# A row transform and an inverse product whose tables move from the streamed to the stationary operand, with two turns through device memory

## The chip, the cores and the metric

The kernel runs on one core of a Trainium2 chip. The metric is device time in microseconds (us); less is better. Engines are named as the profile names them: PE is the matrix engine (PEld its weight loads), DVE the vector engine, ACT the scalar engine, POOL the general engine, SP the engine that here issues most DMAs (SPq its queue).

## The reference

For each of 64 images of 96 channels and 56 x 56 pixels, three layers run one after the other:

```
L0 conv:  1x1 expand to 192, BN, SiLU, shift, shuffle; depthwise 3x3 + identity, SiLU;
          squeeze-excite gate; 1x1 project to 96, BN, + x, SiLU            -> t
L1 attn:  LayerNorm over channels, h = relu(BN(LN(t) @ w1.T))               (3136 tokens x 192)
          X = fft(h over the 3136 tokens, ortho)
          Xr' = relu(Xr*rd - Xi*id + rb) etc. (per channel, shrunk),  y = ifft(..).real
          t = t + BN(y @ w2.T)
L1 ffn:   LayerNorm, fp8 (e5m2) quantised 96 -> 384 -> 96 with fp16 accumulation, + t
```

The transform of length 3136 is done as 56 x 56: a transform along one index of 56 (the row transform, step `f1`), a product with a table that holds the twiddles and the second transform (`f2`), the per-channel part, the product with `w2`, and then the inverse in two steps, `i1` and `i2`. Because the input is real, only NK = 29 of the 56 first frequencies are kept.

## The kernel before

One image is one batch `b` of the plan, and all of its work is cut into small steps (`ea_mm`, `dw_mm`, `f1_mm`, ...). A step is a Python function `step(b, i)` that issues a few instructions. `PLAN` holds a time for every step and part; at the end of the kernel the pairs (batch, step) of all 64 batches are sorted by `b * PERIOD + when`, and issued in that order. The numbers in `PLAN` are therefore only an order; every engine then takes its own instructions strictly in that order, and waits where an operand is not ready. One period holds steps of three or four different batches: the convolution of batch b+1 (`ea`, `eb`, `dw`, `pj`, `c`), the transform of batch b (`w1`, `f1`, `f2`, `w2`, `i1`, `i2`), and the normalisation and the quantised layer of batches b-1 and b-2 (`n`, `x`, `h`, `o`).

The steps that the change touches, in the order of the data:

- `w1_mm`, `w1_ev` (L649, L661): product with `w1` on PE, then DVE writes `relu` times the row scale into `buf_h`, seen as `h_v`.
- `f1_mm`, `f1_ev` (L676, L688): row transform. A slice of `buf_h` of one channel (128 partitions x 56 columns) is the stationary operand, the table `f_tab` (58 columns) is streamed. There are 6 parts of 16 x 2 products. The result comes out turned, with the other pixel index on the partitions, and ACT copies it into `buf_g`, seen as `g_v`.
- `f2_mm`, `f2_u`, `f2_s`, `f2_r`, `f2_p`: the second transform with `l_tab` (L703, L713), then ACT and DVE work; the result goes to `buf_h` as `pq_a` and `pq_b`.
- `w2_mm`, `w2_ev` (L768, L780, L798): product with `w2`; ACT writes `buf_g` as `u_v`.
- `i1_mm`, `i1_ev` (L809, L820): inverse product. Slices of `u_v` (112 x 32) are stationary, `inv_tab` (56 columns) is streamed, in 3 parts of 64 products; ACT copies the turned result into `buf_h` as `p_v`.
- `i2_mm`, `i2_ev` (L831, L844): second inverse product with `r_tab`, added to `t`.

`buf_h` and `buf_g` exist once, so `w1` of the next batch can write only after `i2` of this batch has read. PSUM tiles of these steps alternate between two buffers (`mix_ps`); the other steps share four (`psb`). SP issues the loads of the next image (`x_in`, L192), the output stores (`o_st`, L932) and one small row copy (`sp_ev`, L635).

## Time and profile before

| | |
|---|---|
| time, median of 3 runs | 7428.37 us (7425.02 to 7429.1) |
| span of the profiled execution | 7414.7 us, clock 0.993 |
| PE busy | 7188.3 us (97%), 177666 instructions |
| PEld busy | 5229.7 us (71%) |
| DVE, ACT, POOL busy | 4842.3 (65%), 4641.4 (63%), 1589.9 us (21%) |
| chain that ended last | PE 93%, ACT 3%, issue 3%, DVE 1% |
| DMA | 185.34 MB, mean 25 GB/s |
| `f1_mm` on PE (L676) | 24576 matmuls, 675.6 us |
| `i1_mm` on PE (L809) | 24576 matmuls, 373.3 us, 99.3 us idle before |
| `f1_ev` on ACT (L688), `i1_ev` (L820) | 388.8 us, 176.2 us |

The span runs from the first to the last instruction of one profiled execution; the time of a run lies 13.7 us above it, for what lies around. Busy time of a group is the time in which at least one of its instructions ran; matmuls overlap, so it is far less than the count times the duration of one. "Idle before" is the time for which the engine stood still just ahead of instructions of that group, with the one that ended the wait behind the arrow.

### The profile page before, as it was taken

The numbers are of one execution on the slowest core, as the hardware profiler recorded it, in microseconds if no ns is written. First come the engines' busy times: TensorE is split into PE (matmuls) and PEld (weight loads), VectorE is DVE, ScalarE is ACT, GpSimd is POOL, SyncE is SP. The second block draws the span as 40 slices with busy tenths as digits, with TensorE's granted clock in tenths as the row PEclk, the third lists the DMA queues.
The fourth block names the chain that finished last, engine by engine and source line by source line (L and its number), as shares of the span: only waits on it lengthen the run. The fifth ranks groups of instructions, "written<-read, shape, count | busy, mean of one in ns | idle before, by whom it ended". The sixth has DMA issues, their size and how long they took to land.

```text
span 7414.7 us, 383547 instructions
## 1 busy us (share of the span) xinstructions
PE 7188.3 (97%) x177666; PEld 5229.7 (71%) x177666; DVE 4842.3 (65%) x8790; ACT 4641.4 (63%) x9806; POOL 1589.9 (21%) x1366
## 2 busy tenths in 40 slices
PE   7999999999999999999999999999999999999997
PEld 5777777777777777777777777777777777777775
DVE  5666667666666666666666666666666666666674
ACT  3566666566665666666656666566666666666665
POOL 1221222212212122122121221221212212212222
PEclk9999999999999999999999999999999999999998
DMA  2010110110101101011011011110110111101100
GB/s 52 18 28 20 28 27 19 28 24 23 28 20 28 26 20 28 21 27 28 18 29 26 20 28 23 25 27 19 30 26 20 28 23 24 28 20 28 27 20 21
DMA packets 424334, 185.34 MB, mean 25 GB/s; under 512 B 378786, under 2 KB 422042, under 8 KB 422474
## 3 DMA queue, kind: packets, MB, share of 16 engines
q1 hardware_dynamic: 420794, 159.01, 9.3%
q8 instruction: 1392, 22.81, 1.3%
q0 software_dynamic: 528, 1.50, 0.1%
q14 instruction: 212, 1.73, 0.1%
q10 hardware_dynamic: 1408, 0.28, 0.0%
HBM read 82.80 MB, written 77.07 MB: 22 GB/s over the span
## 4 chain that ended last, share of the span: by engine, by line
PE 93%; ACT 3%; issue 3%; DVE 1%; POOL 0%; DMA 0%; POOLq 0%; ACTq 0%; SPq 0%
PE ps_d L469 14%; PE psa L676 9%; PE psa L649 9%; PE ps_ea L406 5%; PE ps_eb L423 5%; PE psa L831 5%; PE ps_n L580 5%; PE ps_pj L555 5%; PE psa L768 5%; PE psa L809 4%; PE ps_c L580 4%; PE psa L703 4%; PE ps_h L888 4%; PE ps_o L910 3%; PE psa L713 3%
## 5 line engine op out<-in xcount | busy, mean ns | idle before, releaser
L926 POOL TENSOR_TENSOR o<-t,o 112x448 f32<-112x448 f32 x448 | 659.1, 1471 | 3629.9 <-DVE o L920 2280.0
L469 PE MATMUL ps_d<-e_a,diag 32*32 32x392 f32 x36864 | 1029.5, 498 | 0.7 <-ACT d L479 0.7
L898 DVE TENSOR_SCALAR y<-y,qb 128x448 f16<-128x448 f16 x1344 | 483.1, 384 | 761.5 <-ACT y L893 748.4
L491 DVE SCALAR_TENSOR_TENSOR d_last<-e_b,taps,d_last 128x1568 f32<-128x1568 f32 x512 | 972.5, 1899 | 9.3
L469 PEld LDWEIGHTS ps_d<-e_a,diag 32*32 32x32 f32 x36864 | 659.8, 103 | 299.6 <-issue 37.5
L591 DVE TENSOR_REDUCE v<-sq 112x4 f32<-112x384 f32 x896 | 490.6, 548 | 480.7 <-ACT sq L587 479.7
L893 ACT CAST y<-ps_h 128x448 f16<-128x448 f32 x1344 | 682.6, 543 | 165.7 <-PE ps_h L888 157.8
L860 POOL TENSOR_TENSOR rs<-v,mhalf 112x4 f32<-112x4 f32 x448 | 489.5, 1097 | 1264.2 <-DVE v L592 1264.2
L649 PEld LDWEIGHTS psa<-w1c,t 112*64 112x64 f32 x14336 | 609.0, 137 | 178.0 <-issue 86.4
L904 ACT CAST h<-y 128x448 fp8e5<-128x448 f16 x1344 | 733.0, 570 | 2.2 <-DVE y L898 2.0
L676 PEld LDWEIGHTS psa<-f_tab,buf_h 128*56 128x56 f32 x24576 | 650.4, 131 | 111.0 <-ACT buf_g L688 45.4
L649 PE MATMUL psa<-w1c,t 112*64 112x96 f32 x14336 | 688.4, 249 | 3.4 <-DVE buf_h L661 1.8
L676 PE MATMUL psa<-f_tab,buf_h 128*56 128x58 f32 x24576 | 675.6, 216 | 1.1 <-DVE buf_h L661 1.1
L609 POOL TENSOR_TENSOR rs<-v,mhalf 112x4 f32<-112x4 f32 x448 | 461.1, 1034 | 917.2 <-DVE v L592 763.3
L566 DVE TENSOR_TENSOR ps_pj<-ps_pj,x 112x392 f32<-112x392 f32 x512 | 260.6, 566 | 546.0 <-issue 326.1
L572 ACT ACTIVATE t<-ps_pj,pjbn_b 112x392 f32<-112x392 f32 x512 | 289.6, 621 | 413.5 <-DVE ps_pj L566 413.5
L661 DVE SCALAR_TENSOR_TENSOR buf_h<-psa,rs_full 128x768 f32<-128x768 f32 (+1 forms) x512 | 430.8, 852 | 148.7 <-PE psa L649 148.7
L688 ACT COPY buf_g<-psa 128x464 f32<-128x464 f32 x768 | 388.8, 551 | 186.4 <-PE psa L676 184.7
L411 ACT ACTIVATE e_a<-ps_ea 128x448 f32<-128x448 f32 x448 | 237.6, 551 | 427.3 <-PE ps_ea L406 427.2
L809 PE MATMUL psa<-inv_tab,buf_g 112*32 112x56 f32 x24576 | 373.3, 214 | 99.3 <-issue 97.5
L809 PEld LDWEIGHTS psa<-inv_tab,buf_g 112*32 112x32 f32 x24576 | 327.5, 110 | 197.5 <-issue 196.3
L866 DVE TENSOR_TENSOR xt<-ps_n,rs 112x384 fp8e5<-112x384 f32 x448 | 243.7, 556 | 315.8 <-POOL rs L860 311.4
(176 smaller groups left out, 12984.4 us busy)
## 6 DMA issues: line engine op xcount, KB each, us to landing
x<-in_x SPq DMA_DIRECT2D x896, 84.0 KB, 2.7
out_dram<-o SPq DMA_DIRECT2D x896, 84.0 KB, 2.1
l_tab<-in_tab_l SPq DMA_DIRECT2D x1, 1624.0 KB, 6.9
r_tab<-in_tab_r SPq DMA_DIRECT2D x1, 1568.0 KB
t<-dev_t SPq DMA_DIRECT2D x64, 7.0 KB, 1.8
t<-dev_t SPq DMA_DIRECT2D x64, 5.2 KB
ex_row_p<-in_expand_row POOLq DMA_DIRECT2D x1, 336.0 KB, 4.3
s_p<-in_bn POOLq DMA_DIRECT2D x1, 288.0 KB, 4.6
```

The costliest lines, as they stand in the source:

```text
L469: nc.tensor.matmul(pss[r][j * 32 : j * 32 + 32], lhsT=diag[pr, tap, :], rhs=e_a[pr, r0 : r0 + PJ, dx : dx + HW], start=tap == 0, stop=tap ...
L491: nc.vector.scalar_tensor_tensor(d_last, win, w, d_last, ALU.mult, ALU.add)
L580: nc.tensor.matmul(cen[c0:c1, k, 0:C], lhsT=t_of(b)[:, n0 + c0 : n0 + c1], rhs=center, start=True, stop=True)
L591: nc.vector.tensor_reduce(v, sq, AX.X, ALU.add)
L649: nc.tensor.matmul(ps[hc * 64 : hc * 64 + 64, k, 0:C], lhsT=t[:, n0 : n0 + 64], rhs=w1c[:, hc * C : hc * C + C], start=True, stop=True,)
L676: nc.tensor.matmul(ps[r * 64 : r * 64 + HW, k, 0 : 2 * NK], lhsT=buf_h[:, n0 : n0 + HW], rhs=f_tab[:, r, :], start=True, stop=True,)
L809: nc.tensor.matmul(ps[p0 : p0 + 32, k, 0:HW], lhsT=u_v[:, oh * 48 + o, :], rhs=inv_tab[:, r, :], start=True, stop=True,)
L860: nc.gpsimd.tensor_tensor(rs, held.pop(("nv", b, g)), mhalf[0:CP, 0:4], ALU.pow)
L893: nc.scalar.copy(y16, held.pop(("h", b, i)))
L898: nc.vector.tensor_scalar(y16, y16, qb1[:, i % 3 : i % 3 + 1], 0.0, ALU.add, ALU.max)
L904: nc.scalar.copy(held["h8", b, j][:, m, :], held.pop(("y", b, i)), saturate=False)
L926: nc.gpsimd.tensor_tensor(o32, rows, o16, ALU.add)
```

## The change

In `f1` and `i1` the operands trade places: the table becomes the stationary operand and the data are streamed, in `f1` as 7 parts of 4 products of 384 columns on four 64 x 64 corners of the array, in `i1` as 3 parts of 2 products of up to 480 columns on the whole array. The results then do not come out turned. They are turned by writing them to device memory and reading them back: `f1_ev` copies into a new tile `fs` (two buffers), `f1_st` stores it in four DMAs per part, and `f2_ld` loads it into `g_v` in four pieces of four DMAs; `i1_ev` copies into `q_v`, `i1_st` stores it in three DMAs, and `i2_ld` loads `p_v` in two pieces of four DMAs. Ahead of each piece but the first, SP issues a DMA of 4 bytes out of the piece before into a tile `probe`, so that SP waits until that piece has landed. `i2_mm` covers other rows in a part (its count of matmuls is the same), and `r_tab` has another layout of half the size per partition. All times of `PLAN` are new. The one-time loads that POOL issued are issued by ACT. Core of the diff:

```diff
-PERIOD = 116.1319138
+PERIOD = 116.1300000
...
+    "ea_mm": (-134.0591300, -135.8943500, -134.9482400, -82.9315800, -134.3902000, -81.6978800, -73.0405500),
...
+    "dw_mm": (-79.0431300, -76.9247100, -76.4118400, -66.0765200, -63.9181200, -60.6314000),
...
-    "f1_mm": (21.4014670, 24.1096820, 21.6576037, 26.6862219, 27.4741769, 27.9467307),
...
-    "f2_mm": (32.9716451, 29.2956139, 40.4533546, 44.1808546, 54.3439615, 55.8928972),
...
+    "f1_mm": (4.3575000, 6.7899600, 13.2490100, 13.3480500, 26.4222100, 27.3651600, 36.3461700),
+    "f1_ev": (9.9199800, 12.6915700, 15.0915200, 16.8658800, 27.4890500, 27.9876900, 37.4188100),
+    "f1_st": (12.3906800, 15.6355123, 15.8052200, 21.7471100, 30.3743500, 31.4346249, 40.2672500),
+    "f2_ld": (40.4725800, 42.9361900, 44.9466800, 53.7646300),
+    "f2_mm": (40.5122600, 47.0136900, 49.7942100, 50.7436500, 57.9144900, 60.3104800),
...
-    "i1_mm": (80.9444124, 84.7640673, 88.5170591),
-    "i1_ev": (82.2893126, 88.4629084, 91.9656135),
-    "i2_mm": (95.7640245, 96.2774235, 108.3942264, 108.5026333),
...
+    "i1_mm": (78.3167100, 79.8851600, 87.9770000),
+    "i1_ev": (80.3238500, 81.9603700, 83.6106300, 83.8193600, 90.1147200, 90.0279800),
+    "i1_st": (86.9858500, 89.0839200, 95.7684200),
+    "i2_ld": (103.0982000, 105.5906800),
+    "i2_mm": (104.3956884, 104.6307600, 109.4537598, 109.0033800),
...
+    dram = ctx.enter_context(tc.tile_pool(name="dram", bufs=2, space=bass.MemoryType.DRAM))
...
-        nc.gpsimd.dma_start(out=b[0:rows], in_=src.rearrange("(o f) c -> o f c", o=1).to_broadcast([rows, 4, n]))
+        nc.scalar.dma_start(out=b[0:rows], in_=src.rearrange("(o f) c -> o f c", o=1).to_broadcast([rows, 4, n]))
...
-    buf_g = const.tile([128, NK * MID], F32, name="buf_g")
+    buf_g = const.tile([128, (NK + 32) * C], F32, name="buf_g")
...
...
         d, j0, n = W1[g]
         ps = held.pop(("w1", b, g))
         nc.vector.scalar_tensor_tensor(
-            h_v[:, :, d * NJ + j0 : d * NJ + j0 + n],
-            ps[:, 0:n, 0:C].rearrange("p b c -> p c b"),
+            h_v[:, d * NJ + j0 : d * NJ + j0 + n, :],
+            ps[:, 0:n, 0:C],
             0.0,
-            rs_full[:, d, j0 : j0 + n].unsqueeze(1).to_broadcast([128, C, n]),
+            rs_full[:, d, j0 : j0 + n].unsqueeze(2).to_broadcast([128, n, C]),
             ALU.max,
             ALU.mult,
         )
 
 
     def f1_mm(b, g):
-        ps = mix_ps(c=16, k=64)
-        for k in range(16):
-            n0 = (g * 16 + k) * HW
-            for r in range(2):
+        ps = mix_ps(h=2, n=512)
+        for hc in range(2):
+            for d in range(2):
+                n0 = d * NJ + g * 4
                 nc.tensor.matmul(
-                    ps[r * 64 : r * 64 + HW, k, 0 : 2 * NK],
-                    lhsT=buf_h[:, n0 : n0 + HW],
-                    rhs=f_tab[:, r, :],
+                    ps[d * 64 : d * 64 + 64, hc, 0 : 4 * C],
+                    lhsT=f_tab[hc * 64 : hc * 64 + HW, :],
+                    rhs=h_v[hc * 64 : hc * 64 + HW, n0 : n0 + 4, :],
                     start=True,
                     stop=True,
                 )
         held["f1", b, g] = ps
 
-    def f1_ev(b, n):
-        g, hc = divmod(n, 2)
-        c0 = hc * C + g * 16
-        nc.scalar.copy(
-            g_v[:, :, c0 : c0 + 16],
-            held["f1", b, g][:, :, hc * NK : hc * NK + NK].rearrange("p c k -> p k c"),
-        )
+    def f1_ev(b, g):
+        fs = work.tile([128, 4, 2, C], F32, tag="fs", name="fs")
+        ps = held.pop(("f1", b, g))
+        nc.scalar.copy(fs.rearrange("p b h c -> p h b c"), ps[:, :, 0 : 4 * C].rearrange("p h (b c) -> p h b c", c=C))
+        held["fs", b, g] = fs
+
+    def f1_st(b, g):
+        if ("spec", b) not in held:
+            held["spec", b] = dram.tile([4, NJ, 32, MID], F32, tag="spec", name="spec")
+        fs = held.pop(("fs", b, g)).rearrange("p b h c -> p b (h c)")
+        for p in range(4):
+            nc.sync.dma_start(
+                out=held["spec", b][p, g * 4 : g * 4 + 4].rearrange("b k c -> k b c"), in_=fs[p * 32 : p * 32 + 32]
+            )
+
+    LD = ((0, 8), (8, 16), (16, 24), (24, NK))
+
+    def f2_ld(b, i):
+        k0, k1 = LD[i]
+        if i:
+            nc.sync.dma_start(out=probe[0:1, 0:1], in_=g_v[64:65, LD[i - 1][0], 0:1])
+        for r in range(2):
+            for d in range(2):
+                p0 = r * 64 + d * NJ
+                nc.sync.dma_start(out=g_v[p0 : p0 + NJ, k0:k1, :], in_=held["spec", b][d * 2 + r, :, k0:k1, :])
 
 
     F2 = ((fa, pq_a, 0, 8), (fb, pq_b, 0, 8), (fa, pq_a, 8, 8), (fa, pq_a, 16, 8), (fb, pq_b, 8, 7), (fa, pq_a, 24, 5))
...
         if len(low) == len(high) == 4:
             parts = [(ps.rearrange("p u k o -> p (u k) o")[:, :, 0:C], 8)]
         for src, n in parts:
-            nc.scalar.copy(u_v[:, :, at : at + n], src.rearrange("p k o -> p o k"))
+            nc.scalar.copy(u_v[:, at * C : (at + n) * C].rearrange("p (k o) -> p k o", o=C), src)
             at += n
 
 
     def i1_mm(b, g):
-        ps = mix_ps(o=16, b=64)
-        for k in range(16):
-            o = g * 16 + k
-            for oh in range(2):
-                for r in range(2):
-                    p0 = oh * 64 + r * 32
-                    nc.tensor.matmul(
-                        ps[p0 : p0 + 32, k, 0:HW],
-                        lhsT=u_v[:, oh * 48 + o, :],
-                        rhs=inv_tab[:, r, :],
-                        start=True,
-                        stop=True,
-                    )
+        ps = mix_ps(u=2, n=512)
+        for u in range(2):
+            c0 = (g * 2 + u) * 5 * C
+            c1 = min(c0 + 5 * C, NK * C)
+            nc.tensor.matmul(
+                ps[0:CP, u, 0 : c1 - c0],
+                lhsT=inv_tab.rearrange("p r n -> p (r n)"),
+                rhs=u_v[:, c0:c1],
+                start=True,
+                stop=True,
+            )
         held["i1", b, g] = ps
 
-    def i1_ev(b, g):
-        ps = held.pop(("i1", b, g))
-        nc.scalar.copy(p_v[:, :, g * 16 : g * 16 + 16], ps[:, :, 0:HW].rearrange("p o b -> p b o"))
+    def i1_ev(b, n):
+        g, u = divmod(n, 2)
+        c0, c1 = n * 5 * C, min((n + 1) * 5 * C, NK * C)
+        nc.scalar.copy(q_v[:, c0:c1], held["i1", b, g][0:CP, u, 0 : c1 - c0])
+
+    def i1_st(b, g):
+        if ("rows", b) not in held:
+            held["rows", b] = dram.tile([CP, 32 * C], F32, tag="rows", name="rows")
+        cs = slice(g * 10 * C, (g * 10 + 10 if g < 2 else 32) * C)
+        nc.sync.dma_start(out=held["rows", b][:, cs], in_=q_v[:, cs])
+
+    def i2_ld(b, h):
+        ns = slice(h * 14, h * 14 + 14)
+        if h:
+            nc.sync.dma_start(out=probe[0:1, 1:2], in_=p_v[0:1, 0, 0:1])
+        for d in range(2):
+            for r in range(2):
+                p0 = d * 64 + r * 32
+                src = held["rows", b][r * HW : r * HW + HW].rearrange("(n d) (k o) -> d k n o", d=2, o=C)
+                nc.sync.dma_start(out=p_v[p0 : p0 + 32, ns, :], in_=src[d, :, ns, :])
 
 
     def i2_mm(b, g):
         ps = mix_ps(u=2, k=8, a=64)
         for turn in range(2):
             for k in range(7):
-                for bk in range(2):
-                    oh = turn ^ bk
-                    n2 = g * 14 + bk * 7 + k
-                    pr = slice(oh * 64, oh * 64 + 64)
+                for d in range(2):
+                    oh = turn ^ d
+                    pr = slice(d * 64, d * 64 + 64)
                     nc.tensor.matmul(
-                        ps[oh * 64 : oh * 64 + 48, bk, k, 0:HW],
-                        lhsT=buf_h[pr, n2 * 48 : n2 * 48 + 48],
-                        rhs=r_tab[pr, n2, :],
+                        ps[oh * 64 : oh * 64 + 48, d, k, 0:HW],
+                        lhsT=p_v[pr, g * 7 + k, oh * 48 : oh * 48 + 48],
+                        rhs=r_tab[pr, g * 7 + k, :],
                         start=True,
                         stop=True,
                     )
         held["i2", b, g] = ps
 
     def i2_ev(b, n):
-        g, bk = divmod(n, 2)
-        n0 = (g * 14 + bk * 7) * HW
-        cols = t_of(b)[:, n0 : n0 + 7 * HW].rearrange("p (k a) -> p k a", a=HW)
-        nc.vector.scalar_tensor_tensor(cols, held["i2", b, g][0:CP, bk, 0:7, 0:HW], b2_sh, cols, ALU.add, ALU.add)
+        g, d = divmod(n, 2)
+        cols = t_of(b)[:, 0:NPIX].rearrange("p (n d a) -> p n d a", d=2, a=HW)[:, g * 7 : g * 7 + 7, d, :]
+        nc.vector.scalar_tensor_tensor(cols, held["i2", b, g][0:CP, d, 0:7, 0:HW], b2_sh, cols, ALU.add, ALU.add)
 
...
-    f = np.zeros((128, 2, 2 * NK))
+    f = np.zeros((128, 64))
...
-    r = np.zeros((128, HW, HW))
+    r = np.zeros((128, NJ, HW))
...
-    nc = bacc.Bacc("TRN2", target_bir_lowering=False, num_devices=1)
+    nc = bacc.Bacc("TRN2", target_bir_lowering=False, num_devices=1, dynamic_dma_scratch_size=2048)
```

## The prediction, made before the changed kernel ran

> **What bounds the kernel now.** I read the page's first part, then its chain, then the groups kept apart by shape. PE is busy for 97% of the span and 93% of the chain that ended last, and no slice is thin:

> ```profile
> PE 7188.3 (97%) x177666; PEld 5229.7 (71%) x177666; DVE 4842.3 (65%) x8790; ACT 4641.4 (63%) x9806; POOL 1589.9 (21%) x1366
> ...
> PE 93%; ACT 3%; issue 3%; DVE 1%; POOL 0%; DMA 0%; POOLq 0%; ACTq 0%; SPq 0%
> ```

> So PE work taken out is time won, unless PE then waits. The groups of the two steps that change:

> ```profile
> L676 PE MATMUL psa<-f_tab,buf_h 128*56 128x58 f32 x24576 | 675.6, 216 | 1.1 <-DVE buf_h L661 1.1
> L809 PE MATMUL psa<-inv_tab,buf_g 112*32 112x56 f32 x24576 | 373.3, 214 | 99.3 <-issue 97.5 <-ACT buf_g L798 1.0
> L780 PE MATMUL psa<-w2b,buf_h 64*64 64x96 f32 x3712 | 216.6, 251 | 0.0
> L820 ACT COPY buf_h<-psa 128x896 f32<-128x896 f32 x192 | 176.2, 918 | 7.3 <-PE psa L809 7.3
> ```

> Per batch (of 64) `f1` holds PE for (675.6 + 1.1)/64 = **10.6 us** and `i1` for (373.3 + 99.3)/64 = **7.4 us**. The program writes 192 products per batch for each, the trace has 24576/64 = 384: a float32 product is two passes. What a period is worth comes from the gate product, one per batch: (7229.8 - 64.6)/63 = **113.7 us**:

> ```profile
> L540 DVE SCALAR_TENSOR_TENSOR pw<-gate,pj_w x64: 741/742/744, 64.6 to 7229.8; 128x560 f32<-128x560 f32 x64
> ```

> For prices I read PE's timeline of one period (start, length, line, count); a step costs the distance to the next start:

> ```profile
> 2999.62 7.27 PE L469 MATMUL ps_d<-e_a,diag 32*32 32x392 f32 x256
> 3006.82 1.56 PE L713 MATMUL psa<-l_tab,buf_g 128*64 128x112 f32 x28
> ...
> 3014.47 0.89 PE L780 MATMUL psa<-w2b,buf_h 64*64 64x96 f32 x32
> ...
> 3031.22 1.78 PE L809 MATMUL psa<-inv_tab,buf_g 112*32 112x56 f32 x128
> ...
> 3046.85 0.96 PE L406 MATMUL ps_ea<-x,ex_w 112*32 112x448 f32 x8
> 3047.74 2.19 PE L580 MATMUL ps_c<-center,t 112*64 112x96 f32 x48
> 3049.87 0.96 PE L406 MATMUL ps_ea<-x,ex_w 112*32 112x448 f32 x8
> ```

> A `dw` step (96 passes) is 2.7 us, an `f2` part of 16 products (32 passes) 1.7, `c` 0.71, `ea` 0.89; likewise `h` 0.27, `o` 0.67, `eb` 1.4 and `i2` 2.9.

> [...] the trace agrees in `w2` (L780): without the 0.25 us that a single pass takes, (0.89 - 0.25)/31 = 20.6 ns per pass, so four corners of 96 columns in 83 ns. [...]

> **PE work removed.** `f1`: 7 parts x 2 passes = 14 groups of four corners, 384 columns each. At 83 ns per 96 columns that is 332 ns a group, 14 x 0.332 = 4.7 us, so -5.9 us. `i1`: 6 products over 29 x 96 = 2784 columns, two passes, whole array. The trace has no long float32 stream on the whole array; the pair of column tiles in L713 takes 2 x (1.56 - 0.26)/27 = 96 ns for 112 columns, 0.86 ns a column, so 2 x 2784 x 0.86 = 4.8 us. Upper bound: the 12 weight loads of 112 columns (172 ns each in the `pj` group) show in full, 6.9 us; lower bound 4.4, at the 0.79 ns a column of the `pj` passes on four row tiles (32 in 2.90 us: (2.90 - 0.49)/31 x 4/392). I take 4.8: -2.6 us. `i2` keeps its 224 passes on diagonal corner pairs: 0. Sum **-8.45 us per batch, -541 us**: 7428 becomes 6887 if PE never waits anew.

> **Other engines, beside PE.** ACT: `f1_ev` 6.1 us per batch becomes 7 x 0.81 (the 768-column copy of L798) = 5.7; `i1_ev` 2.75 becomes 5 x 0.58 + 0.5 = 3.4; sum +0.2. DVE: `w1_ev` keeps its elements (953 ns now): 0. Against a period of about 108 us ACT comes to 67%, DVE 70%, still under PE. POOL loses only one-time loads; these move to ACT's queue ahead of the first batch: within 5 us either way.

> **SP and the DMAs.** Now 30 DMAs per batch, then 30 + 28 stores + 16 loads + 3 probes + 3 stores + 8 loads + 1 probe = 89. An issue holds SP 0.42 us (output) to 0.67 us (row copy), so some 42 us of a period plus waits: room. Bytes: 2.75 + 2.49 + 1.38 + 1.38 = 8.0 MB more per batch. Today's queue needs 9.3% x 16 x 7414.7 / 420794 = 26 ns per packet; the some 8000 new packets, most of them larger, at 25 to 110 ns come to 35 us of all engines per batch, against today's 10% busy. Bandwidth doesn't bind; the round trips can.

> ```profile
> x<-in_x SPq DMA_DIRECT2D x896, 84.0 KB, 2.7
> out_dram<-o SPq DMA_DIRECT2D x896, 84.0 KB, 2.1
> l_tab<-in_tab_l SPq DMA_DIRECT2D x1, 1624.0 KB, 6.9
> ```

> **The waits added**, by the new order of `PLAN`. Landing prices: 2.1 us for a store, 2.7 for a strided load; bounds 1.8 (best) and 6.1 us (the longest `x` load).
> (a) *`f1_mm(6)` to `f2_mm(0)`*: copy 1.0, four issues 1.8, landing 2.1, four loads of 172 KB (issue 1.8, the last landing 2.8): **9.5 us**. PE has queued between them `dw_mm(0..2)` = **8.1 us**. Stall 1.4, and 0.5 for SP or ACT being late: 1.9. Bounds 0 and 5.
> (b) *`f2_mm(1)`* needs the second piece. SP stands at the probe till the first has landed, then issues: 0.45 + 1.8 + 2.8 = **5.05 us** per piece. On PE: `f2_mm(0)` 1.7, `o` 0.67, `h` twice 0.54, `ea` 0.89 = **3.8**. Stall 1.2; bounds 0 and 3.
> (c) Third and fourth piece: `f2_mm(1)`, `f2_mm(2)`, `dw_mm(3)` and an `h` are 6.4 us against 5.05; `f2_mm(3)` and two `dw` 7.1 against 5.05 plus `o_st(6)`, 0.9. Stall 0; at a cadence of 7 us, 1.5.
> (d) *`i1_mm(2)` to `i2_mm(0)`*: copies 1.3, issue 0.45, landing of 516 KB 3.8, four loads in runs of 384 B (1.9 + 2.7): **10.2 us**. On PE: six `c` 4.3, four `ea` 3.6, `eb` 1.4, two `h` and two `o` 1.9 = **11.1**. Stall 0; bounds 0 and 4. The second load has 6.9 us of PE work against 5.05: 0.
> (e) `fs` has two buffers: `f1_ev(2)` stands behind the landing of `f1_st(0)`, and ACT with it; `w1_mm(5)` waits for that PSUM buffer. 0.4. `w2_mm(3)` now sits just ahead of `i1_mm(2)`: 0.5.
> Behind the waiting SP stand `x_in`, `o_st` and the row copy: the copy for `w1_mm` has 14 us of `i2` and others ahead of it, the rest more.
> Sum of stalls **4.0 us per batch, +256 us**. The first and last batch have little to lay over the turns: +20 us.

> **Sum**: against the profiled run 7414.7 + 13.7 = 7428.4, which is the median: 7428 - 541 + 256 + 20 = **7163 us**, say 7160 (3.6% less).

> **Rivals.** *Turns fully covered*: ACT and SP run ahead, stalls under 2 us; 6890 to 7030, say 6960. For it: (d) has slack. Against: (a) and (b) are short by my prices. *Turns longer than their cover* (the slower side): PE stands at `f2_mm(0)`, `f2_mm(1)` and `i2_mm(0)`. Stores, loads, probes and PE's own instruction fetch (queue q8, 22.8 MB) share 16 engines; with store-to-load trips of 13 us at both turns and 7 us a piece the stalls are 4.9 + 3.2 + 1.5 + 1.9 + 0.9 = 12.4 us, and 7428 - 541 + 794 + 20 = 7700. It decides from 8.1 us of stalls per batch. For it: `i1` already loses 97.5 us to "issue", and the trips are in series. Against: queues are 10% busy now. *Tiles that don't overlap* (the change doesn't do what it says): corners of `f1` in pairs only cost 9.4 us; 7163 + 300 = 7463. Against it is L780.

> **Chances.** Partly covered 0.50 (7030 to 7320), fully covered 0.18, between 7320 and the old time 0.05; same 0.03; slower 0.24 (turns 0.20, tiles 0.04). A difference of 0.2% is about what a measurement of this kernel can tell from no change. Faster 0.73, same 0.03, slower 0.24. The range 6930 to 7540 leaves out about one in twenty below and one in eight above.

> **What would show it.** Right: 3584 matmuls for `f1` and 768 for `i1`, some 300 us busy each; idle time of PE or PEld ahead of `f2` ended by DMA into `buf_g`, some 200 us, and next to none ahead of `i2`; PE share near 93%; period near 109.5 us. Wrong: `f1` near 600 us (tiles), idle time at `f2` over 400 us (turns), or waits of PE for ACT or DVE in the stretch from `f2` to `w2`, where 36 us of ACT work and 30 of DVE stand beside 34 of PE.

## The result, and the profile after

The changed kernel takes **7387.8 us** (median of 4 runs, 7377.8 to 7396.4), the kernel before beside it 7426.7: a ratio of 0.9947 (95% interval 0.9933 to 0.9961). It is 39 us faster where 265 were forecast: clear of the noise, but the sign is all that came out.

The first two lines are from the first part of the page of the changed kernel, the next from its DMA queues, the last is its chain:

```profile
span 7377.8 us, 300741 instructions
...
PE 6817.4 (92%) x132866; PEld 4575.5 (62%) x132866; DVE 4793.1 (65%) x8790; ACT 4638.9 (63%) x9678; POOL 1524.4 (21%) x1355
...
q1 hardware_dynamic: 984506, 670.40, 37.5%
...
PE 48%; DVE 18%; DMA 15%; ACT 10%; SPq 4%; issue 4%; POOL 2%; POOLq 0%; ACTq 0%; DVEq 0%
```

PE lost 371 us of busy time while the span fell by only 37: the rest is now time in which PE stands. Its share of the chain went from 93% to 48%. The granted clock fell from 0.993 to 0.971, which the prediction had not thought of.

The groups of PE with shapes kept apart (columns as before: count, busy us, mean ns, idle before with what ended it):

```profile
L680 PE MATMUL psa<-buf_h,f_tab 56*64 56x384 f32 x3584 | 349.7, 497 | 1.5 <-DVE buf_h L665 1.4
L829 PE MATMUL psa<-buf_g,inv_tab 112*112 112x480 f32 x640 | 294.9, 575 | 0.2 <-ACT buf_g L820 0.2
L829 PE MATMUL psa<-buf_g,inv_tab 112*112 112x384 f32 x128 | 51.6, 485 | 0.0
L725 PE MATMUL psa<-l_tab,buf_g 128*64 128x112 f32 x7424 | 431.2, 269 | 142.6 <-DMA buf_g<-spec 114.2 <-DVE ue L769 9.4 <-ACT h L939 7.8
L735 PE MATMUL psa<-l_tab,buf_g 128*64 128x112 f32 x3840 | 226.1, 264 | 68.5 <-DMA buf_g<-spec 63.4 <-DVE ue L769 4.3 <-issue 0.3
L867 PE MATMUL psa<-r_tab,buf_h 64*48 64x56 f32 x14336 | 360.8, 215 | 91.9 <-DMA buf_h<-rows 76.0 <-issue 13.0 <-DVE dev L620 1.6
L923 PE MATMUL ps_h<-xq,q 96*128 96x448 fp8e5 x1344 | 454.0, 371 | 115.1 <-ACT o L950 113.6 <-ACT y L928 0.6 <-ACT xq L917 0.6
L790 PE MATMUL psa<-w2a,buf_h 128*64 128x96 f32 x3712 | 423.7, 275 | 8.5 <-DVE ue L769 8.4
```

`f1` (L680) and `i1` (L829) have the forecast counts and nearly the forecast time. `f2` (L725, L735) waits 177.6 us for the first turn, `i2` (L867) 76 for the second. Two lines are new surprises: `h_mm` (L923) waits 113.6 us for ScalarE's `o_ev`, and `w2` (L790) has the same instructions as L768 before, but is busy 423.7 us where that was 364.1:

```profile
L768 PE MATMUL psa<-w2a,buf_h 128*64 128x96 f32 x3712 | 364.1, 251 | 1.6 <-DVE ue L747 1.6
```

One period on PE's timeline shows why (start, length, line, count, wait with its releaser):

```profile
3064.70 7.88 PE L473 MATMUL ps_d<-e_a,diag 32*32 32x392 f32 x273
3072.95 0.89 PE L473 MATMUL ps_d<-e_a,diag 32*32 32x392 f32 x15 [0.37 <-issue]
3075.71 1.75 PE L725 MATMUL psa<-l_tab,buf_g 128*64 128x112 f32 x32 [1.87 <-DMA buf_g<-spec]
...
3082.11 0.99 PE L735 MATMUL psa<-l_tab,buf_g 128*64 128x112 f32 x16 [1.65 <-DMA buf_g<-spec]
3083.03 0.36 PE L923 MATMUL ps_h<-xq,q 96*128 96x448 fp8e5 x1
3083.32 3.06 PE L725 MATMUL psa<-l_tab,buf_g 128*64 128x112 f32 x32
...
3101.89 0.35 PE L923 MATMUL ps_h<-xq,q 96*128 96x448 fp8e5 x1 [1.14 <-ACT o L950]
3102.17 0.43 PE L520 MATMUL ps_se<-red,ep_w 24*32 24x1 f32 x32
...
3105.22 1.55 PE L802 MATMUL psa<-w2b,buf_h 64*64 64x96 f32 x32
...
3112.86 0.89 PE L802 MATMUL psa<-w2b,buf_h 64*64 64x96 f32 x32
```

The 32 passes of L725 take 1.75 us at 3075 and 3.06 at 3083; the 32 of L802 take 1.55 us at 3105, soon after a wait, and 0.89 a little later. The clock record has half clock from 3083.58 to 3086.99 and from 3104.06 to 3107.47, and full clock between.

SP's own timeline over the same turn:

```profile
3059.79 9.18 SPq L700 DMA_DIRECT2D spec<-fs  x11
3069.06 3.18 SPq L713 DMA_DIRECT2D buf_g<-spec  x4
3075.41 0.64 SPq L709 DMA_DIRECT2D probe<-buf_g  x1
3076.10 2.45 SPq L713 DMA_DIRECT2D buf_g<-spec  x4
3081.82 0.60 SPq L709 DMA_DIRECT2D probe<-buf_g  x1
```

From the end of `f1_mm(6)` (3064.8) to `f2_mm(0)` (3075.7) the trip takes 10.9 us over 9.1 us of `dw`; a piece takes 3081.82 - 3075.41 = 6.4 us. Four load issues take 3.18 and 2.45 us.

I split every period (53 of them, away from the ends) by the starts of PE's matmuls in the trace: the time to the next start, less the gap in which none ran, at full clock or in a stretch of half clock, and the gaps put to the step that follows them. In us per batch:

| | period | full clock | half clock | idle | of it `f2` | `i2` | `h` | `eb` | `w2` | `i1` |
|---|---|---|---|---|---|---|---|---|---|---|
| before | 114.10 | 111.42 | 0.45 | 2.24 | 0 | 0 | 0 | 0 | 0 | 1.52 |
| after | 112.97 | 100.85 | 5.05 | 7.06 | 3.07 | 1.22 | 1.81 | 0.74 | 0.04 | 0 |
| no turns (`e1`) | 106.84 | 99.60 | 4.43 | 2.81 | 0.70 | 0 | 2.11 | 0 | 0 | 0 |
| no turns, new ACT order (`e10`) | 104.60 | 101.45 | 1.04 | 2.11 | 0.70 | 0 | 0 | 0 | 1.41 | 0 |
| turns, new ACT order (`e5`) | 111.51 | 101.81 | 3.17 | 6.53 | 2.98 | 1.27 | 0.03 | 0.73 | 1.27 | 0 |

Counting half-clock time at half its length, PE's work fell from 111.65 to 103.38 us (-8.27), the loss to the half clock grew from 0.23 to 2.53 (+2.30), and idle time from 2.24 to 7.06 (+4.82): -1.15, but for rounding the 1.13 us by which the period fell. That is 72 us over 64 batches, of which the two ends of the program give 33 back.

### The profile page after: what moved, and what is told of

The parts are those of the page before. It is cut to its first block, busy times and chain, and to the rows that moved or that the text cites. A ratio compares the mean times of both kernels' runs of the same rounds, so it can differ in the third digit from the quotient of the medians.

```text
span 7377.8 us, 300741 instructions
## 1 busy us (share of the span) xinstructions
PE 6817.4 (92%) x132866; PEld 4575.5 (62%) x132866; DVE 4793.1 (65%) x8790; ACT 4638.9 (63%) x9678; POOL 1524.4 (21%) x1355
## 3 DMA queue, kind: packets, MB, share of 16 engines
q1 hardware_dynamic: 984506, 670.40, 37.5%
q14 instruction: 258, 2.11, 0.1%
## 4 chain that ended last, share of the span: by engine, by line
PE 48%; DVE 18%; DMA 15%; ACT 10%; SPq 4%; issue 4%; POOL 2%; POOLq 0%; ACTq 0%; DVEq 0%
DMA buf_g<-spec 7%; PE psa L790 5%; PE psa L653 5%; PE ps_pj L559 5%; PE psa L867 4%; PE psa L829 4%; DVE s L766 4%; DVE ue L769 4%; DMA buf_h<-rows 4%; PE ps_n L584 3%; PE ps_eb L427 3%; PE psa L802 3%; ACT ue L750 3%; DMA spec<-fs 3%; PE ps_c L584 2%
## 5 line engine op out<-in xcount | busy, mean ns | idle before, releaser
L961 POOL TENSOR_TENSOR o<-t,o 112x448 f32<-112x448 f32 x448 | 614.7, 1378 | 4114.1 <-DVE o L955 1565.3
L473 PE MATMUL ps_d<-e_a,diag 32*32 32x392 f32 x36864 | 1075.3, 497 | 3.6 <-issue 3.4
L895 POOL TENSOR_TENSOR rs<-v,mhalf 112x4 f32<-112x4 f32 x448 | 450.5, 1010 | 1195.1 <-DVE v L596 1190.5
L928 ACT CAST y<-ps_h 128x448 f16<-128x448 f32 x1344 | 679.0, 542 | 12.7 <-PE ps_h L923 10.7
L725 PE MATMUL psa<-l_tab,buf_g 128*64 128x112 f32 x7424 | 431.2, 269 | 142.6 <-DMA buf_g<-spec 114.2
L923 PE MATMUL ps_h<-xq,q 96*128 96x448 fp8e5 x1344 | 454.0, 371 | 115.1 <-ACT o L950 113.6
L613 POOL TENSOR_TENSOR rs<-v,mhalf 112x4 f32<-112x4 f32 x448 | 443.7, 1012 | 539.5 <-DVE v L596 536.9
L779 DVE SCALAR_TENSOR_TENSOR buf_h<-ue,s 128x448 f32<-128x448 f32 (+2 forms) x768 | 478.9, 665 | 111.8 <-ACT s L773 111.8
L725 PEld LDWEIGHTS psa<-l_tab,buf_g 128*64 128x64 f32 x7424 | 377.3, 141 | 266.9 <-issue 134.7
L766 DVE SCALAR_TENSOR_TENSOR s<-psa,fa,ue 128x448 f32<-128x448 f32 (+1 forms) x512 | 324.9, 635 | 273.9 <-ACT ue L750 273.9
L591 ACT ACTIVATE sq<-ps_n 112x384 f32<-112x384 f32 x448 | 221.4, 494 | 390.0 <-PE ps_n L584 389.0
L750 ACT ACTIVATE ue<-psa,fa 128x448 f32<-128x448 f32 (+1 forms) x512 | 330.6, 684 | 192.6 <-PE psa L725 119.2
```

Source lines behind the costliest of these rows:

```text
L473: nc.tensor.matmul(pss[r][j * 32 : j * 32 + 32], lhsT=diag[pr, tap, :], rhs=e_a[pr, r0 : r0 + PJ, dx : dx + HW], start=tap == 0, stop=tap ...
L725: nc.tensor.matmul(ps[c0 : c0 + 64, k, 0:CP], lhsT=g_v[:, k1, c0 : c0 + 64], rhs=l_tab[:, k1, :], start=True, stop=True,)
L750: nc.scalar.activation(held["ue", b, i][:, q, 0:n, :], held["f2", b, i][:, 0:n, 0:HW], AF.Identity, bias=par[:, 2 + q : 3 + q], scale=par[ ...
L766: nc.vector.scalar_tensor_tensor(held["s", b, i][:, q, 0:n, :], im, par[:, m : m + 1], a, ALU.mult, ALU.add)
L779: nc.vector.scalar_tensor_tensor(pq[:, k0 : k0 + n, q * HW : q * HW + HW], ue[:, q, 0:n, :], 0.0, s[:, q, 0:n, :], ALU.max, op)
L923: nc.tensor.matmul(ps, lhsT=q1[:, m * 128 : (m + 1) * 128], rhs=held["xq", b][:, rows, :], start=True, stop=True)
```

## The experiments

**Were the turns the cost, or something that goes with the new order?** `e1_noturn` leaves the DMAs of both turns out:

```diff
     def f1_st(b, g):
+        held.pop(("fs", b, g))
+        return
...
     def f2_ld(b, i):
+        return
...
     def i1_st(b, g):
+        return
...
     def i2_ld(b, h):
+        return
```

> Leaves out all stores and loads of both turns (f1_st, f2_ld, i1_st, i2_ld issue nothing; f2 and i2 read what lies in buf_g and buf_h, so the output is not the reference's). Theory 'turns': the change took out 7.9 us of PE work per batch (f1 10.6 to 5.2, i1 7.4 to 4.85) and lost it again to the waits of PE at the turns and to the lower clock that follows them; without the turns the time is 7427 - 64 x 7.9 = 6920, some 6880 to 6980, at a clock of 0.99. Rival 'ACT and DVE': the stretch from f2 to w2 is bound by ACT and DVE, and the time stays above 7150.

Measured: 6963.4 us, ratio to before 0.9388 (0.9374 to 0.9402). So the turns cost 424 us, and the saved PE work is real. (Without the turns the later steps work on stale values; `f1` and `i1` take as long there as in the changed kernel, 5.16 and 4.86 us a batch.) The time is as expected, the clock is not, 0.974 instead of 0.99, and one wait stayed:

```profile
PE ps_h L928 <- ACT o L955: 131.5, 63, 2.2
```

This is from its waits of PE (total us, times, longest us): L928 is `h_mm`. ScalarE is late there without any turn, and 4.43 us of half clock a batch is left too.

**What in the turns?** `e2_static` takes away the wait of the loads for the stores, by loading what batch 0 stored (in `i2_ld` likewise, from `rows`); `e3_noprobe` takes away the probes, so that SP issues all pieces at once.

```diff
-                nc.sync.dma_start(out=g_v[p0 : p0 + NJ, k0:k1, :], in_=held["spec", b][d * 2 + r, :, k0:k1, :])
+                nc.sync.dma_start(out=g_v[p0 : p0 + NJ, k0:k1, :], in_=held["spec", 0][d * 2 + r, :, k0:k1, :])
```

> All stores, loads and probes are kept, but every batch loads what batch 0 stored (so the output is wrong after batch 0): a load no longer waits for a store of its own batch. Theory 'turns', idle time only: the waits ahead of f2_mm(0) (1.9 us) and of i2_mm(0) (0.6) go, 7388 - 64 x 2.5 = 7228. Theory 'turns and clock': about half of the time at half clock goes too, about 7130. Rival 'it shows up elsewhere' (the next wait takes its place): above 7340.

```diff
-        if i:
-            nc.sync.dma_start(out=probe[0:1, 0:1], in_=g_v[64:65, LD[i - 1][0], 0:1])
...
-        if h:
-            nc.sync.dma_start(out=probe[0:1, 1:2], in_=p_v[0:1, 0, 0:1])
```

> The four probe DMAs per batch are left out, so the pieces of a load follow each other at once; the output is the reference's. Theory 'turns', idle time only: the waits ahead of f2_mm(1) (1.65 us) and of the second half of i2 (1.1) go, 7388 - 64 x 2.75 = 7212. With the clock: about 7110. Rival 'flood': 2.5 MB of loads in one burst hold up other transfers, PE's instruction fetch among them, and 'issue' idle time grows: 7388 or slower.

Measured: 7274.0 us (0.9804, 0.9787 to 0.9820) and 7355.8 (0.9922, 0.9901 to 0.9944). Waiting for the stores is worth 114 of the 424 us, less than the theory's 160, and it is won at the other turn than expected. SP's waits in the changed kernel, then PE's groups in `e2_static`:

```profile
SPq L857 <- DMA rows<-buf_g: 233.8, 68, 4.7
SPq L713 <- DMA spec<-fs: 44.7, 83, 2.6
...
L725 PE MATMUL psa<-l_tab,buf_g 128*64 128x112 f32 x7424 | 425.4, 267 | 118.8 <-DMA buf_g<-spec 95.1 <-ACT h L939 7.7 <-DVE ue L769 6.4
L735 PE MATMUL psa<-l_tab,buf_g 128*64 128x112 f32 x3840 | 226.4, 264 | 71.9 <-DMA buf_g<-spec 68.4 <-DVE ue L769 3.0
L867 PE MATMUL psa<-r_tab,buf_h 64*48 64x56 f32 x14336 | 342.0, 215 | 26.8 <-DMA buf_h<-rows 19.3 <-issue 6.0 <-DVE dev L620 1.2
```

`i2` (L867) waits 19.3 us for DMAs instead of 76.0, `f2` (L725, L735) still 163.5 instead of 177.6. In the first turn SP is hardly held up by the stores: it comes to the loads late, because it issues four stores and then four loads one after another (from 3065.81 to 3072.24 in the period above), and these stay in `e2_static`.

In the changed kernel SP waits for the stores before it issues the loads (the 233.8 and 44.7 us of L857 and L713 above); that it has to was an assumption of the forecast and was not shown. By `e2_static` this waiting has a price of 1.8 us a batch, about a quarter of what the turns cost. The expectation for `e3_noprobe` was far too high: the wait of `f2` for DMAs falls from 177.6 to 129.3 us, but one of 40.0 us for DVE's `f2_s` takes most of its place.

**Which turn?** `e11_nof` has only the edits of `e1_noturn` in `f1_st` and `f2_ld`, `e12_noi` only those in `i1_st` and `i2_ld`.

> The first turn's stores, loads and probe are left out (spec; the second half of the row transform works on what its buffer holds), the second turn (rows) is kept. Theory: the two turns cost about in the ratio of the waits of TensorE at their reading steps, 3.07 to 1.22 us a batch, of the 424 us that both cost: 300 us here, 7388 - 300 = about 7085 us. Rival: what the turns cost is mainly the clock after any wait, so that one turn left costs nearly as much as two: 7200 us or more.

> The second turn's stores, loads and probe are left out (rows; the last product works on what its buffer holds), the first turn (spec) is kept. Theory: by the same ratio 120 us, 7388 - 120 = about 7268 us, and with e11_nof the two gains add up to about 424 us. Rival (the clock after any wait, one turn as dear as two): under 60 us, 7330 us or more.

Measured: 7120.8 us (0.9587, 0.9571 to 0.9603) and 7234.6 (0.9744, 0.9729 to 0.9758). The first turn costs 267 us and the second 153, together 420 against the 424 of both: the costs add. The second turn costs more than its share of the waits.

**Is ScalarE late by the order alone?** Around the wait of `h_mm`, ScalarE's timeline of the changed kernel:

```profile
3098.70 0.69 ACT L750 ACTIVATE ue<-psa,fb 128x392 f32<-128x392 f32 x1
3100.74 0.68 ACT L750 ACTIVATE ue<-psa,fb 128x392 f32<-128x392 f32 x1 [1.35 <-DVE ue L769]
3101.32 0.52 ACT L950 CAST o<-ps_o 112x448 f16<-112x448 f32 x1
```

The second `f2_u` of a part (L750) stands behind DVE's `f2_s` (L769), because both write the tile `ue` and the new table puts `f2_s(8)` (62.298) ahead of `f2_u(9)` (62.346). `o_ev(1)` (L950) stands behind it, and `h_mm(7)` on PE at 3101.89 behind that. `e5_acts` moves three numbers of the table, written here as assignments (which of the three moves does how much was not tried):

```diff
-PLAN["f2_u"][3] = 49.61397
-PLAN["f2_u"][9] = 62.34601
-PLAN["o_ev"][1] = 178.90474
+PLAN["f2_u"][3] = 48.04
+PLAN["f2_u"][9] = 62.295
+PLAN["o_ev"][1] = 177.63
```

> The changed kernel with three numbers of the new PLAN moved, nothing else: f2_u(3) and f2_u(9) ahead of the DVE step f2_s that they now wait for, and o_ev(1) ahead of f2_u(8). Theory 'the new order holds ACT up': PE's wait of 1.8 us per batch ahead of h_mm(7), which is for ACT's o_ev(1) and is there without the turns too, goes, and with it the low clock that follows it (some 4 us per batch in w2, se, pj and h at half clock, worth 2): 7388 - 64 x (1.8 to 3.8), that is 7145 to 7275. Rival 'ACT is simply full there': the wait moves on, 7350 to 7400.

Measured: 7275.3 us (0.9793, 0.9778 to 0.9807), 112 us less than the changed kernel and at the small end of what the theory gave. The wait of `h_mm` (here L1027) is gone; a wait of `w2` (L894) is new, and smaller. From its groups:

```profile
L1027 PE MATMUL ps_h<-xq,q 96*128 96x448 fp8e5 x1344 | 431.4, 360 | 4.5 <-issue 1.7 <-ACT o L1054 1.1 <-ACT y L1032 0.9
L894 PE MATMUL psa<-w2a,buf_h 128*64 128x96 f32 x3712 | 406.6, 268 | 87.5 <-DVE ue L873 87.5
```

The idle time fell by only 0.53 us a batch. The greater part of the gain is clock: half-clock time fell from 5.05 to 3.17, and half of that fall, 0.94 us, is lost time won back.

`e10_acts_nt` makes the same three moves in `e1_noturn`.

> The three moved order numbers of e5_acts with the stores, loads and probes of both turns left out (the second half of each product then works on what its buffer already holds). Theory: ScalarE is late by the order alone, turns or none. The 2.1 us of waits a batch that e1_noturn still had at the head, and some of its 4.4 us of half clock, go: 6963 - 64 x (1.5 to 2.5) = 6800 to 6870 us. Rival: ScalarE's hold-up is a consequence of the turns, and without them the moved numbers bring nothing: 6940 to 6990 us.

Measured: 6825.3 us (0.9190, 0.9176 to 0.9204), 138 us less than `e1_noturn`, at a clock of 0.989. ScalarE's lateness is thus a cost of the new order, apart from the turns. The chip was not the one of `e1_noturn`, but the kernel before differs by only 8 us between the two. Again idle time fell by 0.70 us (45 us in all) and half clock by 3.39, of which half, 1.7 us, is lost time. Put in a row, these runs divide the result: 7427 - 602 (the change without turns and without ScalarE's lateness) = 6825, + 138 (ScalarE's place in the order) = 6963, + 424 (turns) = 7388. In the other order the shares differ a little: with the turns in place ScalarE's lateness costs 112 us (`e5_acts`), and the turns then 450.

**More cover for the turn?** `e6_cover` moves work that is there anyway between `f1_mm(6)` and the parts of `f2`: `o`, `h`, `ea` and two more `h` ahead of `f2_mm(0)`, and one `dw` each ahead of `f2_mm(1)` and `f2_mm(3)`, with the steps on ScalarE that belong to them.

```diff
-PLAN["f2_mm"][0] = 40.51226
-PLAN["h_mm"][8] = 164.07852
-PLAN["dw_mm"][3] = -66.07652
-PLAN["dw_mm"][4] = -63.91812
+PLAN["f2_mm"][0] = 43.45
+PLAN["h_mm"][8] = 159.53
+PLAN["dw_mm"][3] = -72.53
+PLAN["dw_mm"][4] = -65.83
...
```

> The changed kernel with f2_mm(0) issued after o, two h and ea, and dw_mm(3) ahead of f2_mm(1), dw_mm(4) ahead of f2_mm(3) (with the ACT steps that these need): the same work and the same DMAs, more PE work over the turn. Theory 'turns': the waits ahead of f2 fall from 3.1 to about 1 us per batch, 7388 - 64 x 2 = 7260. Rival 'the chain through the buffers is as long as the period': the waits turn up later, 7350 to 7400.

Measured: 7403.7 us (0.9972, 0.9961 to 0.9983), no gain over the changed kernel. The DMA waits at `f2` did go (178 us to about 10), and this took their place (the line before `f2_mm(4)`, and from the waits of PE the total):

```profile
3108.67 2.78 PE L839 MATMUL psa<-l_tab,buf_g 128*64 128x112 f32 x28 [2.81 <-DVE ue L873]
```

```profile
PE psa L839 <- DVE ue L873: 162.6, 64, 4.3
```

L839 is `f2_mm` with `l_tab` in four quarters, L873 the second half of `f2_s`. Once the turn has landed, `f2` goes no faster than ScalarE and DVE take its parts in their order of steps; from the end of `f1_mm(6)` to `f2_mm(4)` it is 30.1 us here and 31.6 in the changed kernel. Either engine is busy for some 12 of the last 18 us, so another order of their steps might shorten the chain; none was tried. Cover placed ahead of this chain moved the wait along it.

`e7_both` has the moves of `e5_acts` and `e6_cover`, `e8_both_np` also leaves the probes out, and `e9_acts_np` is `e5_acts` without probes.

> The moves of e5_acts and e6_cover together. If the two waits are separate, the gains add: some 7100. If one hides the other, no better than the better of the two.

> e7_both without the probes. Theory 'turns': the piece-by-piece cadence of 6.4 us no longer sets f2_mm(1) and the second half of i2; 64 x 1 to 2 us below e7_both, some 7000. Rival 'flood': loads in one burst hold up PE's instruction fetch and the first piece; no gain over e7_both.

> The three moved order numbers of e5_acts, and both probes left out as in e3_noprobe; the whole computation is done. If the probes' own cost (32 us with the old order) is separate from ScalarE's hold-up, the time is 7275 - 32 = about 7243 us. Rival: once ScalarE is no longer late, loads that are issued without waits between them only land out of turn with the stores and the weights, as in e8_both_np against e7_both (+21 us), and the time is 7275 to 7300 us.

Measured: 7330.9 us (0.9869, 0.9855 to 0.9884), 7352.2 (0.9897, 0.9882 to 0.9912) and 7258.7 (0.9761, 0.9732 to 0.9791). The cover takes back half of what `e5_acts` won: the gains neither add nor leave the better of the two. Without probes `e7_both` becomes some 21 us slower, as the rival said. `e9_acts_np` is the fastest version with nothing left out, but its interval overlaps that of `e5_acts`: whether the probes cost anything there is open. Either beats both kernels by 1.5% or more.

**Does the clock fall through PE's waits?** `e4_warm` fills the three waits with small products whose result is never read: 14 ahead of `f2_mm(0)`, 12 ahead of `f2_mm(1)`, 8 ahead of `h_mm(7)`.

```diff
+            nc.tensor.matmul(out, lhsT=eye, rhs=l_tab[0:CP, 0, 0:64], start=True, stop=True)
```

> Small extra matmuls (64 columns, into columns of PSUM that nothing reads) ahead of f2_mm(0) (14), f2_mm(1) (12) and h_mm(7) (8), where PE waits; the output is the reference's. They add work and take no wait away. Theory 'turns and clock': the clock stays up, the mean rises from 0.971 towards 0.99, and f2 and w2 run at full speed: 7388 less 64 x 1.5 to 3 us, 7200 to 7290. Theory 'idle time only': no gain, 7388 to 7420, since the extra matmuls only fill the waits or lengthen them.

Measured: 7476.2 us (1.0081, 1.0063 to 1.0099), a miss. The products were sized for the 4.7 us of waits and took 7.0 us a batch (0.2 us each), more than there was to fill:

```profile
L723 PE MATMUL psa<-l_tab,eye 112*112 112x64 f32 x4336 | 455.9, 262 | 0.0
```

Half-clock time did fall, from 5.05 to 2.64 us a batch, with the idle time (7.06 to 3.20). That agrees with the waits as a cause of the lower clock, but the run can't price it.

## Why the prediction was wrong

**PE work removed: right in kind, a little high in size.** `f1` went from 10.36 to 5.17 us a batch (-5.2, forecast -5.9): a group of four corners of 384 columns takes 5.17/14 = 369 ns, not 332. `i1` went from 7.14 (its idle time with it) to 4.86 (-2.3, forecast -2.6); 0.87 ns a column, as taken from L713. The rival that tiles don't overlap is out: one of the four passes alone takes 497 ns (L680). What I priced at nothing gained: the other steps together lost 2.3 us of PE work and 0.7 of idle time, though nothing in them changed (`ea` 6.23 to 5.56, `w1` 10.24 to 9.70, `o` 4.65 to 4.07). They stand elsewhere in the order, and PE has some 45000 fewer passes to take; which of the two made them dearer before was not tried. In all 10.5 us went where 8.45 were forecast. Without the 3.0 us of the other steps (192 us in all) the change would have been a loss by these sums: that the sign came out right is luck.

**The waits added: this is the step that failed.** The forecast sum was 4.0 us of stalls, from the turns and two small waits; there are 7.06 us of idle time. The largest term that it lacks is PE's wait for ScalarE, which the step "Other engines, beside PE" put at nothing because ScalarE is busy for only 67% of a period. By the terms:

- (a) to (c), `f2`: 3.1 forecast, 3.07 measured, 2.78 of it waits for DMAs (177.6 us over 64 batches). The parts missed both ways, so the good sum is luck in part: the trip took 10.9 us, not 9.5, with a cover of 9.1, not 8.1, and a piece took 6.4, not 5.05. Without the turn a wait of 0.70 us for DVE stands at `f2` (`e1`); in the changed kernel the turn hides most of it (0.21 left).
- (d), `i2`: 0 forecast, 1.22 measured. Trip 11.0 us, not 10.2, and cover 10.2, not 11.1: a margin of 0.9 us became a lack of 0.8.
- (e): 0.9 forecast, 0.1 measured.
- Not in the sum: `h_mm` 1.81 (ScalarE late), `eb` 0.74 (DVE's `xt`; gone in `e1` and `e11`, so it comes with the first turn).

I compared ACT's and DVE's loads with the period and never followed the order on those engines. The prediction did name waits of PE for ACT or DVE between `f2` and `w2` as what would make it wrong. The wait of `h_mm` lies in that stretch.

**The clock was not in the sum at all.** 2.3 us a batch, about 147 us, are lost at half clock. Half-clock time is 1.04 us a batch with neither the turns nor the late ScalarE (`e10`), 4.43 with ScalarE late alone (`e1`), 3.17 with the turns alone (`e5`) and 5.05 with both. Either brings most of it, so it can't be divided between the two.

**"Bandwidth doesn't bind; the round trips can": partly.** Against `e1` the turns add 6.13 us a batch: 4.25 of idle time, 0.62 of half clock, and 1.25 of full-clock work, of which `dw` 0.72, `i2` 0.33 and `eb` 0.21. This last term was not forecast. `dw` is at 15.97 to 16.03 us without the first turn (`e1`, `e11`) and at 16.65 to 16.69 with it, but traffic as such does not explain it: of the six parts of `dw`, the first takes 0.36 us longer than in `e1` while the DMA engines are 29% busy, the second only 0.02 at 61%, the third 0.22 at 65%. How the turn lengthens this work stays open. The queue's own share, 37.5%, is near what was forecast (9.3%, and 35 of some 110 us, together 41%).

**Sum**: -10.5 (work) + 7.06 (idle) + 2.3 (clock) = -1.1 us a batch, -72 us, and +33 at the ends (forecast +20) give the 39 us measured. By the runs, the change without its two costs takes out 602 us, where 541 less 20 at the ends were forecast (the prediction's two terms, 5.9 and 2.6, make 8.5, not 8.45; 3 us in all). The turns cost 424 us where 256 were forecast, and ScalarE's place in the order 138 where nothing was. These three misses, 81 the good way and 168 and 138 the other, are the 225 us between forecast and result. The turns' idle time alone, 4.25 us a batch, is near the 4.0 forecast; what was left out of their price is the added work, the clock and the ends. The rival *turns longer than their cover* had 12.4 us of stalls, three times what the turns bring.

## What to carry to other kernels

When a change reorders a whole kernel, follow each engine's own order from the bottleneck's waits backward, not its busy share: here three numbers in a table cost 112 to 138 us, a quarter to a third of the round trips through memory. Price a short wait on the matrix engine above its length, since clock may go with it (in `e5_acts` 0.53 us less idle time came with 0.94 us less lost to half clock); and before covering a long transfer, see what chain starts where it lands, for cover that only delays that chain brought nothing here.

## What the hardware showed unexpectedly

The half-clock stretches last 3.41 us or whole multiples of it, but for one of 50.1 us at the end of the program (of 86 in the changed kernel, 61 are 3.41, 22 are 6.83 and 2 are 10.24 us). Half clock followed waits shorter than one such stretch: PE waited 1.14 us for the `h_mm` at 3101.89, half clock began at 3104.06, and no wait of `h_mm` was longer than 2.3 us. Around that wait stand L505, L520 and L528, products of one column (54 passes in some 1.1 us).
